# Scores and outputs in four 64x64 quarters of the array, whole-array work in six blocks of a batch

## The chip, the cores and the metric

One core of a Trainium2 chip. The metric is the device time of one execution in microseconds (us), median of several. Every run below fell in the fast state. Names of bursts: attention works through each batch in 16 **bursts**, u=0 to u=15, of two score tiles each; four **groups** of four bursts make a batch, one for each pair of heads and half of the queries. Names of tiles: `ps` holds scores, `p` their exponentials, `po` a group's outputs, `den` its denominators, `drow` a copy of them, `dcol` what is read back of them from DRAM; `c` is the column means in DRAM, `crow` their broadcast. A **step** is a piece of the next batch's work on TensorE (two graph matmuls, or a tile of keys or values).

## The reference, cut to what matters

Two layers, each with a residual and a layernorm. The change touches only the attention of the first, over 16 batches of 1024 nodes with 256 channels and 4 heads of 64, all in fp32:

```python
c_adj = jnp.mean(fea, axis=1)                      # column means of x
diff = c_adj[:, None, :] - c_adj[:, :, None]
A = jnp.abs(jnp.abs(jax.nn.sigmoid(diff) - 0.5) - 0.5) * 2.0
Wg = adj[None] * (A + A.T) * 0.5                   # the kernel: Abs, Tanh, times adj
g = relu(einsum('bcn,bnm->bcm', fea, Wg) * para)   # "graph": gives q
kv = x @ kv_w                                      # keys and values
attn = softmax(einsum('bhnd,bhmd->bhnm', q, k) * scale)
out = einsum('bhnm,bhmd->bhnd', attn, v)
x = layernorm(x + out)                             # then a graph layer, untouched here
```

## The kernel before

While a batch is in attention, the next batch's keys, values, graph products and weights (Abs/Tanh) are made beside it. The parts that matter (cuts marked):

```python
def begin():                      # once a batch: column means
    # ... csum = sum of x on VectorE, ccol and ncol from it
    nc.sync.dma_start(c_d[b].rearrange("o (n p) -> p (o n)", p=P), ncol)       # 1024 values of 4 bytes
    nc.sync.dma_start(s["crow"], c_d[b][0].partition_broadcast(P))

def graph_mm(c, half, part):      # ... 2 of 8 matmuls into pg
    if part == 3:
        nc.vector.scalar_tensor_tensor(q, ps, -scale, para_s[:, c, hs], op0=ALU.mult, op1=ALU.mult)
        nc.scalar.activation(q, q, AF.Relu)

def scores(i):                    # 64 rows x 128 columns of the array, two heads abreast
    for hd in range(2):
        r = slice(hd * D, (hd + 1) * D)
        nc.tensor.matmul(ps[:, hd * HALF : (hd + 1) * HALF], kT[r, pr, m * P : (m + 1) * P],
                         qT[r, pr, qh * HALF : (qh + 1) * HALF], start=True, stop=True)
    nc.scalar.activation(p, ps, AF.Exp)

def outputs(i):                   # 128 rows x 64 columns; acc is the sum of the p on VectorE
    # ...

def normalise(b, pr, qh):         # once a group: denominators
    # ... den = ones x acc, on TensorE
    nc.scalar.copy(row, den)
    for hd in range(2):
        nc.sync.dma_start(den_d[k][hd : hd + 1, :], row[hd * D : hd * D + 1, :])
    for hd in range(2):
        nc.sync.dma_start(col[:, :, hd], den_d[k][hd : hd + 1, :].rearrange("o (n p) -> p (o n)", p=P))
    nc.vector.reciprocal(r_all[:, k], col)

with tc.manual_schedule(engines={mybir.EngineType.PE}):
    for j in range(len(bursts)):
        # ... scores of j; one or two steps of the next batch; outputs of j - 1
```

The last statement matters below: only TensorE's instructions keep the order of the program. The order of the other engines, and of the DMAs that they issue, is laid out when the kernel is built.

Of the kernel before, what the change touches and what calls it, by code (L numbers as in the profile page):

```python
# [10 lines left out]
F32 = mybir.dt.float32  # L11
# [7 lines left out]
P = 128  # L19
HALF = 512  # L20
# [495 lines left out]
def fast_path(  # L516
# [42 lines left out]
    def tile_o(name):  # L559
        return ps_o.tile([P, HALF], F32, tag="o", name=name)  # L560
# [52 lines left out]
    with (  # L613
# [146 lines left out]
        def scores(i):  # L760
            b, pr, qh, m = units[i]
            qT, kT = st[b]["qT"], st[b]["kT"]
            ps = tile_s(f"ps_{i}")
            for hd in range(2):
                r = slice(hd * D, (hd + 1) * D)
                nc.tensor.matmul(  # L766
                    ps[:, hd * HALF : (hd + 1) * HALF], kT[r, pr, m * P : (m + 1) * P],
                    qT[r, pr, qh * HALF : (qh + 1) * HALF], start=True, stop=True,
                )
            p = pp.tile([P, N], F32, tag="p", name=f"p_{i}")  # L770
            nc.scalar.activation(p, ps, AF.Exp)  # L771
            A[i] = p

        def outputs(i):
            b, pr, qh, m = units[i]
            s, p = st[b], A.pop(i)
            if m == 0:
                G[b, pr, qh] = {
                    "po": tile_o(f"po_{i}"),
                    "acc": accp.tile([P, N], F32, tag="acc", name=f"acc_{i}"),  # L780
                }
            g = G[b, pr, qh]
            for hd in range(2):
                h = 2 * pr + hd
                nc.tensor.matmul(  # L785
                    g["po"][hd * D : (hd + 1) * D, :], s["v"][:, m, h * D : (h + 1) * D],
                    p[:, hd * HALF : (hd + 1) * HALF], start=(m == 0), stop=(m == NCH - 1),
                )
            if m == 0:
                g["p0"] = p  # L790
            elif m == 1:
                nc.vector.tensor_add(g["acc"], g.pop("p0"), p)
            else:
                nc.vector.tensor_add(g["acc"], g["acc"], p)  # L794

        def normalise(b, pr, qh):

            g = G[b, pr, qh]
            k = (b * PAIRS + pr) * 2 + qh
            den = tile_t(f"den_{k}")  # L800
            for hd in range(2):
                nc.tensor.matmul(
                    den[hd * D : (hd + 1) * D, :], ones,
                    g["acc"][:, hd * HALF : (hd + 1) * HALF], start=True, stop=True,
                )
            row = rdp.tile([P, HALF], F32, tag="drow", name=f"drow_{k}")
            nc.scalar.copy(row, den)
            for hd in range(2):
                nc.sync.dma_start(den_d[k][hd : hd + 1, :], row[hd * D : hd * D + 1, :])
            col = small.tile([P, 4, 2], F32, tag="dcol", name=f"dcol_{k}")  # L810
            for hd in range(2):
                nc.sync.dma_start(
                    col[:, :, hd], den_d[k][hd : hd + 1, :].rearrange("o (n p) -> p (o n)", p=P)
                )
            nc.vector.reciprocal(r_all[:, k], col)
            g["oT"] = op.tile([P, HALF], F32, tag="oT", name=f"oT_{k}")
            nc.scalar.copy(g["oT"], g["po"])

        def residual(b, pr, qh):
            g, s = G.pop((b, pr, qh)), st[b]  # L820
# [22 lines left out]



        BURST = 2
        bursts = [range(i, i + BURST) for i in range(0, len(units), BURST)]
        PERB = PER // BURST
        with tc.manual_schedule(engines={mybir.EngineType.PE}):
# [5 lines left out]
                run(steps, 2)  # L855
            next_first, next_steps, next_side = prologue(1)
            run(next_first, 4)
            full, cols64 = {}, {}

            def back(j):  # L860

                run(cols64.get(j, []), 9)
                for i in bursts[j]:
                    outputs(i)
                b, pr, qh, m = units[bursts[j][-1]]
                if m == NCH - 1:
                    cols64.setdefault(j + 1, []).append((normalise, (b, pr, qh)))
                    full.setdefault(j + 5, []).append((residual, (b, pr, qh)))

            for j in range(len(bursts)):  # L870
                b, u = j // PERB, j % PERB
                for i in bursts[j]:
                    scores(i)
                if u == 0:
                    steps, side = next_steps, next_side
                    next_first, next_steps, next_side = [], [], []
                run(full.get(j, []), 9)
                if u == 5 and b + 2 < B:
                    load_x(b + 2)
                    next_first, next_steps, next_side = prologue(b + 2)  # L880
                run(side, 3)
                run(steps, 1 + u % 2)
                if u >= 10:
                    run(next_first, 1)
                if u == PERB - 1:
                    run(steps, 99)
                if j:
                    back(j - 1)
            j = len(bursts)
            back(j - 1)  # L890
            for k in range(j, j + 6):
                run(cols64.get(k, []), 9)
                run(full.get(k, []), 9)

        top = l0c.tile([P, 2], F32, name="top")
# [276 lines left out]
```

## Time and profile before

| | before |
|---|---|
| time, median (range) | 2955.81 us (2954.03 to 2958.54) |
| TensorE busy | 2788.7 us, 94% |
| attention: first scores to last output transpose | 1754.3 us |
| in it: TensorE idle / changes of array shape | 11.5 us / 755 |

The last two rows are counted from the single TensorE records of the trace: the length between two records, the gaps between their ends and starts, and how often the recorded rows and columns change from one matmul to the next. The lines of the page stand in the prediction. The traced execution took 2962.3 us, a little over the range of the others, as it needed 89.0 us before the first scores (the trace after: 79.9); the comparisons of traces below are therefore of attention alone.

Two lines of the view of waits of the kernel before are needed later (engine, line, what it waited for; us in total, times, longest): ScalarE's relu of q waiting for VectorE's multiply, and VectorE's reciprocal waiting for the load of the denominators, which is next to nothing.

```profile
ACT qT L706 <- DVE qT L703: 136.5, 35, 7.1
DVE r_all L815 <- DMA dcol<-den: 3.8, 6, 1.9
```

### The profile page before, as it was taken

How to read it: one execution, taken by the hardware profiler on the slowest of the kernel's cores; microseconds unless marked ns; L12 is line 12 of the kernel's file. 1: busy time of each engine (PE TensorE's matmuls, PEld its weight loads, DVE VectorE, ACT ScalarE, POOL GpSimd, SP SyncE). 2: the span in 40 equal slices, each digit the busy share in tenths (PEclk: the TensorE clock that was granted, in tenths of full speed). 3: DMA queues.
4: the chain of work that ended last, by engine and by line, in shares of the span. 5: the costliest groups of instructions: out<-in, count | busy, mean ns of one | idle time of the engine just before them, and what ended most of it. 6: DMA issues, size and time to landing. Idle time of an engine off the chain costs nothing. (4 is left out here: it accounts for less than half of the span.)

```text
span 2960.4 us, 23733 instructions
## 1 busy us (share of the span) xinstructions
PE 2788.7 (94%) x9170; PEld 1178.5 (40%) x9170; DVE 1345.3 (45%) x2002; ACT 1143.4 (39%) x1313; POOL 222.8 (8%) x196
## 2 busy tenths in 40 slices
PE   5999999999999999999999999899999999999842
PEld 3433333333333333333333432644444444344432
DVE  3455654654654555655555646412111121333464
ACT  2553553553553553553554534001110111233383
POOL 0001001001001000100100101000000000000032
PEclk8999999999999999999999999699999999999955
DMA  4001101101101001001011011022212121243265
GB/s 135 8 1 36 29 8 36 30 8 36 29 8 37 29 8 37 16 21 37 8 29 36 1 35 38 29 85 114 85 57 86 71 85 57 104 165 142 85 213 200
DMA packets 122026, 168.42 MB, mean 57 GB/s; under 512 B 86704, under 2 KB 103600, under 8 KB 111664
## 3 DMA queue, kind: packets, MB, share of 16 engines
q1 hardware_dynamic: 112720, 99.70, 11.1%
q0 software_dynamic: 9184, 67.12, 5.7%
q8 instruction: 74, 1.21, 0.2%
q14 instruction: 48, 0.39, 0.0%
HBM read 99.36 MB, written 67.44 MB: 56 GB/s over the span
## 5 line engine op out<-in xcount | busy, mean ns | idle before, releaser
L771 ACT ACTIVATE p<-ps 128x1024 f32<-128x1024 f32 x512 | 497.5, 1020 | 406.2 <-PE ps L766 406.0
L794 DVE TENSOR_TENSOR acc<-acc,p 128x1024 f32<-128x1024 f32 x384 | 469.4, 1222 | 394.7 <-ACT p L771 377.6
L766 PE MATMUL ps<-qT,kT 64*128 64x512 f32 x2048 | 509.0, 615 | 0.1
L785 PE MATMUL po<-p,v 128*64 128x512 f32 x2048 | 492.5, 602 | 0.0
L697 PE MATMUL pg<-wg,x 128*128 128x512 f32 x1024 | 481.0, 606 | 2.8 <-ACT kT L718 2.6
L984 PE MATMUL pagg<-ahT,x1l 128*128 128x512 f32 x1024 | 444.1, 593 | 0.0
L1003 ACT ACTIVATE hw<-ph,col_b 128x1024 f32<-128x1024 f32 x64 | 71.3, 1114 | 651.4 <-PE ph L999 651.4
L766 PEld LDWEIGHTS ps<-qT,kT 64*128 64x128 f32 x2048 | 176.1, 186 | 327.7 <-issue 264.4
L984 PEld LDWEIGHTS pagg<-ahT,x1l 128*128 128x128 f32 x1024 | 194.4, 191 | 241.1 <-issue 241.1
L697 PEld LDWEIGHTS pg<-wg,x 128*128 128x128 f32 x1024 | 182.8, 190 | 269.4 <-issue 264.5
L785 PEld LDWEIGHTS po<-p,v 128*64 128x64 f32 x2048 | 129.8, 136 | 288.5 <-issue 288.2
L833 POOL TENSOR_TENSOR x<-x,o 128x512 f32<-128x512 f32 x64 | 118.2, 1846 | 1604.4 <-DVE o L828 1604.4
L1063 PE MATMUL po<-hl,w2T 128*128 128x512 f32 x512 | 222.8, 598 | 6.9 <-ACT hl L1054 6.9
L999 PE MATMUL ph<-agg,w1T 128*128 128x512 f32 x512 | 222.2, 592 | 0.0
L988 DVE COPY agg<-pagg 128x1024 f32<-128x1024 f32 x32 | 39.2, 1224 | 377.8 <-PE pagg L984 377.8
L685 DVE SCALAR_TENSOR_TENSOR wg<-wg,adj_s 128x1024 f32<-128x1024 f32 x128 | 157.0, 1248 | 74.8 <-ACT wg L684 74.8
L679 ACT ACTIVATE wg<-crow,ccol 128x1024 f32<-128x1024 f32 x128 | 141.2, 1141 | 35.5 <-PE pg L697 23.6
L1005 DVE BATCH_NORM_STATS2 bn_st<-hw 128x6 f32<-128x512 f32 x128 | 82.3, 685 | 152.4 <-ACT hw L1003 152.4
L1063 PEld LDWEIGHTS po<-hl,w2T 128*128 128x128 f32 x512 | 98.3, 192 | 131.5 <-issue 121.9
L999 PEld LDWEIGHTS ph<-agg,w1T 128*128 128x128 f32 x512 | 97.3, 190 | 122.5 <-issue 122.5
L1094 PE MATMUL pf<-ident,o 128*128 128x128 f32 x256 | 62.4, 421 | 83.4 <-DVE xf L1099 56.5
L727 PE MATMUL pv<-kvw_s,xT 128*128 128x256 f32 x512 | 126.5, 391 | 13.3 <-DMA kvw_s<-in_L_gnn_kv_w_dram 10.3
(85 smaller groups left out, 1855.3 us busy)
## 6 DMA issues: line engine op xcount, KB each, us to landing
h<-hw POOLq DMA_DIRECT2D x16, 2048.0 KB, 6.5
hl<-h SPq DMA_DIRECT2D x16, 2048.0 KB
x<-in_x_dram SPq DMA_DIRECT2D x16, 1024.0 KB
x<-x POOLq DMA_DIRECT2D x16, 1024.0 KB, 4.3
x1l<-x SPq DMA_DIRECT2D x16, 1024.0 KB
xf<-x SPq DMA_DIRECT2D x16, 1024.0 KB
out_dram<-xf POOLq DMA_DIRECT2D x16, 1024.0 KB, 5.4
crow<-c SPq DMA_DIRECT2D x16, 512.0 KB
```

The source lines that it names most:

```text
L679: nc.scalar.activation(w, s["crow"], AF.Abs, bias=s["ccol"][:, n : n + 1])
L685: nc.vector.scalar_tensor_tensor(w, w, 1.0, adj_s[:, n, :], op0=ALU.subtract, op1=ALU.mult)
L697: nc.tensor.matmul(ps, xt[:, n, c * P : (c + 1) * P], s["wg", n][:, hs], start=(n == 0), stop=(n == NCH - 1),)
L727: nc.tensor.matmul(pt[:, j * C : (j + 1) * C], s["xT"][:, c, n * P : (n + 1) * P], kvw_s[:, c, C : 2 * C], start=(c == 0), stop=(c == CC - 1),
L766: nc.tensor.matmul(ps[:, hd * HALF : (hd + 1) * HALF], kT[r, pr, m * P : (m + 1) * P], qT[r, pr, qh * HALF : (qh + 1) * HALF], start=True, ...
L771: nc.scalar.activation(p, ps, AF.Exp)
L785: nc.tensor.matmul(g["po"][hd * D : (hd + 1) * D, :], s["v"][:, m, h * D : (h + 1) * D], p[:, hd * HALF : (hd + 1) * HALF], start=(m == 0) ...
L794: nc.vector.tensor_add(g["acc"], g["acc"], p)
L833: nc.gpsimd.tensor_tensor(xs, xs, o.rearrange("p n h d -> p n (h d)"), ALU.add)
L984: nc.tensor.matmul(ps[:, hs], xt[:, m, c * P : (c + 1) * P], ahT[:, m, hs], start=(m == 0), stop=(m == NCH - 1),)
L999: nc.tensor.matmul(ps[:, hs], w1T[:, c, k * P : (k + 1) * P], t[:, c, hs], start=(c == 0), stop=(c == CC - 1),)
L1063: nc.tensor.matmul(ps[:, hs], w2T[:, k, c * P : (c + 1) * P], ht[:, k, hs], start=(k == 0), stop=(k == HC - 1),)
```

## The change

The intent: TensorE pays for changes between array shapes, so make scores, outputs and denominators one shape (64x64, four quarters at once), and put the work that needs the whole array into six blocks of a batch in place of a piece in every burst. The price is a second half of `den` and `po`, to be added.

```diff
 def scores(i):
-    for hd in range(2):
-        nc.tensor.matmul(ps[:, hd half], kT[r, pr, m * P : (m + 1) * P], ...)
+    for kh in range(2):
+        for hd in range(2):
+            ks = slice(m * P + kh * D, m * P + (kh + 1) * D)
+            nc.tensor.matmul(ps[kh * D : (kh + 1) * D, hd half], kT[r, pr, ks], ...)
 def outputs(i):                       # the same split; two tiles po[0], po[1]
+    if m == NCH - 1:
+        nc.scalar.copy(g["oT"], g["po"][0])
+        nc.vector.tensor_add(g["oT"], g["po"][1], g["oT"])
 def normalise(b, pr, qh):
-    den = tile_t(f"den_{k}")
+    den = [tile_t(f"den_{k}_{kh}") for kh in range(2)]     # four quarter matmuls
-    nc.scalar.copy(row, den)
+    nc.scalar.copy(row, den[0])
+    nc.vector.tensor_add(row, den[1], row)
+FULL = {1: 4, 4: 4, 6: 4, 9: 4, 11: 4, 14: 4}              # burst: steps of the next batch
 for j in range(len(bursts)):
     # scores(j)
+    run(quarter.get(j, []), 9)                             # normalise, now right after scores
-    run(steps, 1 + u % 2)
+    if u in FULL:
+        run(full.get(j, []), 9)                            # residuals
+        run(steps, FULL[u])
     # outputs(j - 1)
```

(Cut: the matmul arguments, and the placing of the residuals and of the transposes of x.)

More of the change, by code (lines that the diff above doesn't have):

```diff
@@ L763, in scores @@
             ps = tile_s(f"ps_{i}")
-            for hd in range(2):
-                r = slice(hd * D, (hd + 1) * D)
-                nc.tensor.matmul(
-                    ps[:, hd * HALF : (hd + 1) * HALF], kT[r, pr, m * P : (m + 1) * P],
-                    qT[r, pr, qh * HALF : (qh + 1) * HALF], start=True, stop=True,
-                )
+            for kh in range(2):
+                for hd in range(2):
+                    r = slice(hd * D, (hd + 1) * D)
+                    ks = slice(m * P + kh * D, m * P + (kh + 1) * D)
+                    nc.tensor.matmul(
+                        ps[kh * D : (kh + 1) * D, hd * HALF : (hd + 1) * HALF], kT[r, pr, ks],
+                        qT[r, pr, qh * HALF : (qh + 1) * HALF], start=True, stop=True,
+                    )
             p = pp.tile([P, N], F32, tag="p", name=f"p_{i}")
@@ L778, in outputs @@
                 G[b, pr, qh] = {
-                    "po": tile_o(f"po_{i}"),
+                    "po": [tile_o(f"po_{i}_{kh}") for kh in range(2)],
                     "acc": accp.tile([P, N], F32, tag="acc", name=f"acc_{i}"),
@@ L784, in outputs @@
                 h = 2 * pr + hd
-                nc.tensor.matmul(
-                    g["po"][hd * D : (hd + 1) * D, :], s["v"][:, m, h * D : (h + 1) * D],
-                    p[:, hd * HALF : (hd + 1) * HALF], start=(m == 0), stop=(m == NCH - 1),
-                )
+                for kh in range(2):
+                    r = slice(kh * D, (kh + 1) * D)
+                    nc.tensor.matmul(
+                        g["po"][kh][hd * D : (hd + 1) * D, :], s["v"][r, m, h * D : (h + 1) * D],
+                        p[r, hd * HALF : (hd + 1) * HALF], start=(m == 0), stop=(m == NCH - 1),
+                    )
             if m == 0:
@@ L794, in outputs @@
                 nc.vector.tensor_add(g["acc"], g["acc"], p)
+            if m == NCH - 1:
+                k = (b * PAIRS + pr) * 2 + qh
+                g["oT"] = op.tile([P, HALF], F32, tag="oT", name=f"oT_{k}")
+                nc.scalar.copy(g["oT"], g["po"][0])
+                nc.vector.tensor_add(g["oT"], g["po"][1], g["oT"])
         def normalise(b, pr, qh):
@@ L799, in normalise @@
             k = (b * PAIRS + pr) * 2 + qh
-            den = tile_t(f"den_{k}")
+            den = [tile_t(f"den_{k}_{kh}") for kh in range(2)]
             for hd in range(2):
-                nc.tensor.matmul(
-                    den[hd * D : (hd + 1) * D, :], ones,
-                    g["acc"][:, hd * HALF : (hd + 1) * HALF], start=True, stop=True,
-                )
+                for kh in range(2):
+                    r = slice(kh * D, (kh + 1) * D)
+                    nc.tensor.matmul(
+                        den[kh][hd * D : (hd + 1) * D, :], ones[r, :],
+                        g["acc"][r, hd * HALF : (hd + 1) * HALF], start=True, stop=True,
+                    )
             row = rdp.tile([P, HALF], F32, tag="drow", name=f"drow_{k}")
-            nc.scalar.copy(row, den)
+            nc.scalar.copy(row, den[0])
+            nc.vector.tensor_add(row, den[1], row)
             for hd in range(2):
@@ L815, in normalise @@
             nc.vector.reciprocal(r_all[:, k], col)
-            g["oT"] = op.tile([P, HALF], F32, tag="oT", name=f"oT_{k}")
-            nc.scalar.copy(g["oT"], g["po"])
         def residual(b, pr, qh):
@@ L857, in fast_path @@
             run(next_first, 4)
-            full, cols64 = {}, {}
+            full, quarter = {}, {}
             def back(j):
-                run(cols64.get(j, []), 9)
                 for i in bursts[j]:
@@ L866, in back @@
                 if m == NCH - 1:
-                    cols64.setdefault(j + 1, []).append((normalise, (b, pr, qh)))
-                    full.setdefault(j + 5, []).append((residual, (b, pr, qh)))
+                    quarter.setdefault(j + 2, []).append((normalise, (b, pr, qh)))
+                    k = j + 4
+                    while k % PERB not in FULL:
+                        k += 1
+                    full.setdefault(k, []).append((residual, (b, pr, qh)))
             for j in range(len(bursts)):
@@ L876, in fast_path @@
                     next_first, next_steps, next_side = [], [], []
-                run(full.get(j, []), 9)
                 if u == 5 and b + 2 < B:
@@ L881, in fast_path @@
                 run(side, 3)
-                run(steps, 1 + u % 2)
-                if u >= 10:
-                    run(next_first, 1)
-                if u == PERB - 1:
-                    run(steps, 99)
+                if u in FULL:
+                    run(full.get(j, []), 9)
+                    run(steps, FULL[u])
+                    if u >= 9:
+                        run(next_first, 1 if u < 12 else 2)
                 if j:
@@ L890, in fast_path @@
             back(j - 1)
-            for k in range(j, j + 6):
-                run(cols64.get(k, []), 9)
+            for k in range(j, j + 8):
+                run(quarter.get(k, []), 9)
                 run(full.get(k, []), 9)
```

## The prediction

> **What bounds the kernel now.** I read the page first (busy shares, the costliest groups, the idle time in front of each), then the TensorE timeline of one batch in the steady part, then the ScalarE and GpSimd timelines there. The chain that ended last covers only the last 12 us and says nothing of this change.
>
> The page: TensorE is busy in nine tenths or more of nearly every slice, and the two groups that the change rewrites never wait. The last column is the idle time before a group over the whole run.
>
> ```profile
> PE   5999999999999999999999999899999999999842
> PEclk8999999999999999999999999699999999999955
> L771 ACT ACTIVATE p<-ps 128x1024 f32<-128x1024 f32 x512 | 497.5, 1020 | 406.2 <-PE ps L766 406.0
> L766 PE MATMUL ps<-qT,kT 64*128 64x512 f32 x2048 | 509.0, 615 | 0.1
> L785 PE MATMUL po<-p,v 128*64 128x512 f32 x2048 | 492.5, 602 | 0.0
> ```
>
> The reader is to see 0.1 and 0.0 us of idle time: scores (L766) and outputs (L785) are bound by TensorE itself, while the exponential (ScalarE, L771) waited 406 us for it. So only TensorE's own time can be won here, and what other engines gain or lose counts only once they make it wait. Attention runs to about 1840 us of 2956; what follows is untouched.
>
> The timeline of TensorE over one burst with one "step" (columns: start, us, engine, line, operation, count):
>
> ```profile
> 1001.17 1.99 PE L766 MATMUL ps<-qT,kT 64*128 64x512 f32 x8
> 1003.08 1.98 PE L714 MATMUL pk<-xT,kvw_s 128*128 128x512 f32 x4
> 1005.00 1.94 PE L785 MATMUL po<-p,v 128*64 128x512 f32 x8
> 1006.87 1.99 PE L766 MATMUL ps<-qT,kT 64*128 64x512 f32 x8
> ...
> 1036.29 3.70 PE L697 MATMUL pg<-wg,x 128*128 128x512 f32 x8
> 1039.92 1.94 PE L785 MATMUL po<-p,v 128*64 128x512 f32 x8
> ```
>
> Each program matmul of 512 columns is recorded as two passes; within one block the next pass of the same tile starts 0.4295 us after the last (single starts in the trace: 1003.617, 1004.046, 1004.476). Scores and outputs already run two tiles abreast, so each of the three blocks is four rounds, 4 x 0.4295 = 1.718 us. But the starts are 1.91, 1.92 and 1.87 us apart: 5.70 us a burst for 5.154 us of rounds, 0.546 us lost at three changes of array shape (64x128, 128x128, 128x64). The wider block shows the contrast: 8 whole-array matmuls take 3.63 us, 1.71 more than 4 do, so staying in a shape costs nothing. By single starts: the first round after a change comes 0.09 us late, and its weight load delays the second round by 0.05 (64 columns) to 0.10 us (128 columns). **That is 0.19 us into the whole array, 0.145 into 128x64, 0.20 into 64x128.**
>
> A batch takes 112.6 us, from one residual add to the same one a batch later:
>
> ```profile
> 482.12 2.28 POOL L833 TENSOR_TENSOR x<-x,o 128x512 f32<-128x512 f32 x1 [17.29 <-DVE o L828]
> ...
> 594.74 2.31 POOL L833 TENSOR_TENSOR x<-x,o 128x512 f32<-128x512 f32 x1 [17.28 <-DVE o L828]
> ```
>
> Sum of its parts: scores 64 rounds, outputs 64, graph 64, keys 16, values 16, denominators 8 = 232 x 0.4295 = 99.6 us; transposes about 4 x 0.5 + 4 x 0.53 = 4.1; changes of shape 16 x 0.546 = 8.7. Together 112.4, so the account closes.
>
> **What the Trainium skill says.** (1) "TensorEngine Tiling (Array Packing)", Tiling Modes, Key Properties: "Changing tiling mode (not just tile) drains the TensorE". The trace agrees: 0.145 to 0.20 us per change, none between blocks of one shape. (2) "TensorE: Matmul & The Clock Gate", Part 3, Measured speedup vs the span model: tiles abreast cost one matmul plus some 4 ns per further tile. The trace agrees for two tiles (starts 1001.166 and 1001.173, and still 0.429 us to the next round); four tiles no trace here shows. (3) The same page, Part 2, LDWEIGHTS: its time goes with the columns, not the rows. The trace agrees: 186 ns for 64x128, 136 ns for 128x64. (4) "PSUM — Partial Sum Buffer", Specifications: eight banks of 512 fp32. The kernel holds 2 x 2 for scores, 2 for `t`, 2 for `o`: all eight. No trace shows that, but it is why each new double tile takes both buffers of its pool.
>
> **The change, part by part.** *Removed.* Quarters make scores and outputs one shape, and whole-array work stands in six blocks of a batch instead of in every burst. Forty-eight changes of shape a batch (8.7 us) become twelve: 6 x (0.19 + 0.145) = 2.0 us. Saved: 6.7 us a batch. The last batch has no steps, and its bursts take 3.79 us for 3.436 of rounds: 16 x 0.35 = 5.6 us saved less a little for residuals, some 5.
>
> *Unchanged if four tiles run abreast.* A unit's scores and outputs become four quarter matmuls each, still two rounds. Twice as many weight loads, each 64 columns at 0.136 us, beside rounds of 0.43: hidden, as now. Denominators: four quarters abreast, two rounds, as now.
>
> *Added off TensorE.* Per group (four a batch) one more VectorE add from PSUM for `po` and one for `den`, about 0.69 us each (128x512 from PSUM, as L828): 5.5 us on an engine busy 62.6 of 112.6. Hidden as work.
>
> *Added as waits.* (a) `den` now takes both `t` buffers. At u=1 and u=9 a whole-array block follows at once and needs one of them. From the start of the scores: exponentials begin 1.17 us later (1001.17 to 1002.34) and both are done at about 3.05; `den` ends at 1.72 + 0.86 = 2.58 plus 0.2 for its end to be seen, so the ScalarE copy runs 3.05 to 3.6, and TensorE, ready at 2.6, waits until 3.65: **1.1 us**, second buffer 0.1 more. At u=1 ScalarE is also making the next batch's weights, and an Abs or Tanh of 1 us may stand in front: I take 1.7. Sum 2.8 us a batch. (b) The two `po` tiles take both `o` buffers; the next group needs them 1.72 + 0.86 us later (scores and `den` lie between), while copy and add take 0.2 + 0.6 + 0.7 = 1.5. No wait, but for the group that ends at u=3, with the layernorm on VectorE: 0.4. (c) The second transpose of x at u=14 waits for the graph tile, 0.45, in place of today's 0.78 (the TensorE timeline has 0.78 before `den` at 1083.55): 0.3 gained. (d) ScalarE in bursts without a whole-array block: 3.44 us now hold two exponentials (1.85), and sixteen Abs and Tanh (16 us) become possible when the graph matmuls at u=14 free their buffers. The old timeline shows ScalarE mixing them in as soon as buffers come free:
>
> ```profile
> 1093.34 1.91 ACT L771 ACTIVATE p<-ps 128x1024 f32<-128x1024 f32 x2
> 1095.15 2.18 ACT L679 ACTIVATE wg<-crow,ccol 128x1024 f32<-128x1024 f32 x2
> 1097.23 1.99 ACT L684 ACTIVATE wg<-wg 128x1024 f32<-128x1024 f32 x2
> 1099.12 0.62 ACT L706 ACTIVATE qT<-qT 128x512 f32<-128x512 f32 x1
> 1099.64 2.18 ACT L679 ACTIVATE wg<-crow,ccol 128x1024 f32<-128x1024 f32 x2
> 1101.72 1.01 ACT L771 ACTIVATE p<-ps 128x1024 f32<-128x1024 f32 x1
> 1102.63 1.05 ACT L684 ACTIVATE wg<-wg 128x1024 f32<-128x1024 f32 x1
> 1103.57 1.01 ACT L771 ACTIVATE p<-ps 128x1024 f32<-128x1024 f32 x1
> ```
>
> An exponential may come one such operation late (that of 1101.72 did, by 1.1 us). The score buffers give 3.44 - 2.1 = 1.3 us of slack, and the six-block layout leaves ScalarE some 9 us at u=14 before the next exponentials. So nearly hidden: 0.2.
>
> *Sum.* 6.7 - 2.8 - 0.4 + 0.3 - 0.2 = 3.6 us a batch; 15 x 3.6 + 5 = 59 us, less 1 to 2 for two more evictions in the tail: 2956 - 57, about **2899**. I chose 2897, leaning a little to the side that some waits fall into gaps of the others.
>
> **The rivals.** *Waits (a) do not occur, or are shorter,* because the copy of `den` finds ScalarE free: for it, six blocks look placed with care; against it, the exponentials' timing above leaves it no earlier slot. Then 6.3 us a batch, some 2856. *ScalarE becomes the bound between u=14 and u=4:* exponentials queue behind several Abs and Tanh, as the order is fixed beforehand and the bursts got shorter, 3.44 us for 5.7 to 7.4. For it: six of these stand between two pairs of exponentials in the old timeline. Against it: they waited for buffers then, and only an order made for a slower TensorE would keep them so. It would cost 3 to 6 us a batch, so 2930 to 2985. *Four quarters do not run at full rate:* fp32 passes of four tiles start raggedly, or loads of weights collide. Five per cent on 136 quarter rounds of a batch are 2.9 us, 47 us in all: 2945. Against it: two tiles show a stagger of 7 ns and no loss[...]. *VectorE holds `p` too long* at u=4 with a layernorm of some 7 us: four `p` buffers give about 2.5 us of slack; at most 1 us a batch.
>
> **Range and chances.** The gain without new waits is firm (105 us: 2851). What the waits take back is some 45 us with an error about as large, to both sides; half-rate quarters would be far outside, but I hold them unlikely (one in ten for a loss that shows). So 2848 to 2948 eight times in ten. Two per cent is 2896.7 us, nearly my middle: faster 0.52, same 0.43, slower 0.05.
>
> **What would show it.** Right: scores and outputs as 64*64 groups of 4096 records each; pure bursts with starts 3.44 us apart; four starts within some 20 ns per round; TensorE's idle time naming the copy of `den` (L807's successor) before poT at u=1 and u=9, near 1 us each; a batch of about 109 us. Wrong: a round of quarters longer than 0.435 us; score matmuls idle behind the exponential by more than 1 us a batch; or whole-array blocks that lose much more than 0.335 us to their two changes. The prediction fails most likely through ScalarE's order, which I cannot read from the old trace.

## The result, and the profile after

| | before | after |
|---|---|---|
| time, median (range), four runs each | 2955.11 (2954.03 to 2958.54) | 3185.28 (3181.13 to 3186.38) |
| ratio, 95% interval | | 1.0774 (1.0755 to 1.0793): slower |
| attention | 1754.3 us | 1983.6 us |
| TensorE idle in it | 11.5 us | 248.1 us |
| TensorE busy at half clock in it | 0 | 139.1 us |
| changes of array shape | 755 | 189 |
| everything after attention | 1117.1 us | 1115.7 us |

Ratios are the mean time of one kernel's fast runs over that of the other's of the same rounds, so not quite the ratio of the medians quoted. (The kernel before has one run more here than in the first table.)

The page of the kernel after, against the lines in the prediction:

```profile
PEclk9999999998999999999999999969999999999955
L768 PE MATMUL ps<-qT,kT 64*64 64x512 f32 x4096 | 522.5, 621 | 148.7 <-ACT p L773 148.7
L789 PE MATMUL po<-p,v 64*64 64x512 f32 x4096 | 502.5, 603 | 4.9 <-DVE oT L803 4.9
```

The quarters are there, 4096 records each, and their busy time is near the old one's (522.5 and 502.5 us against 509.0 and 492.5). Single starts in the trace show four quarters at full rate: 1100.374, .378, .381 and .384 us, the next round 0.430 us on. But scores, which waited 0.1 us in all, now wait 148.7 us for the exponential.

The waits after, beside the two lines of before:

```profile
ACT qT L706 <- DVE qT L703: 532.5, 49, 19.9
DVE r_all L827 <- DMA dcol<-den: 204.5, 48, 9.9
PE ps L768 <- ACT p L773: 148.7, 53, 10.2
```

The reciprocal's wait went from 3.8 to 204.5 us, that of the relu from 136.5 to 532.5. The timeline of one batch shows how they hang together (start, us, engine, line, operation; in brackets the idle time before it and what ended it; SPq is the DMA queue that SyncE issues to):

```profile
1016.61 2.29 DVE L657 TENSOR_REDUCE csum<-x 128x8 f32<-128x2048 f32 x1 [5.72 <-DMA x<-in_x_dram]
...
1018.82 0.68 DVE L819 TENSOR_TENSOR drow<-den,drow 128x512 f32<-128x512 f32 x1
...
1019.52 0.54 SPq L821 DMA_DIRECT2D den<-drow  x2
...
1020.17 0.39 SPq L662 DMA_DIRECT2D c<-ncol  x1
...
1020.67 1.05 SPq L824 DMA_DIRECT2D dcol<-den  x2
...
1028.72 0.34 SPq L664 DMA_DIRECT2D crow<-c  x1
1031.70 0.20 DVE L827 RECIPROCAL r_all<-dcol 128x8 f32<-128x8 f32 x1 [9.60 <-DMA dcol<-den]
1031.82 0.64 DVE L703 SCALAR_TENSOR_TENSOR qT<-pg,para_s 128x512 f32<-128x512 f32 x1
1032.50 0.63 ACT L706 ACTIVATE qT<-qT 128x512 f32<-128x512 f32 x1 [18.98 <-DVE qT L703]
...
1034.09 3.56 PE L768 MATMUL ps<-qT,kT 64*64 64x512 f32 x16 [9.36 <-ACT p L773]
```

Read it from the bottom. TensorE stood 9.36 us for an exponential. On ScalarE a relu stood in front of it; the relu needed VectorE's multiply; on VectorE the reciprocal stood in front of that; and the reciprocal stood 9.60 us for the denominators, whose load (dcol) had been issued at 1020.67, 11.0 us earlier. Thirteen of the 16 batches have such a stall of TensorE, of 6.0 to 10.2 us, 108.2 of the 148.7 us in all. Two other groups of the same batch get their denominators 2.7 us after the issue (1045.70 to 1048.35, 1078.74 to 1081.48). What is different here is the store of the column means, c<-ncol, issued between the denominators' store and their load. The same stretch of the kernel before has it behind them:

```profile
1032.53 5.10 SPq L812 DMA_DIRECT2D dcol<-den  x2
...
1039.42 0.20 DVE L815 RECIPROCAL r_all<-dcol 128x8 f32<-128x8 f32 x1
...
1039.76 0.36 SPq L662 DMA_DIRECT2D c<-ncol  x1
...
1048.27 0.34 SPq L664 DMA_DIRECT2D crow<-c  x1
```

There, too, c<-ncol needs 8.5 us until the load behind it (crow) can be issued, but nobody else waits.

The other 40.5 us that scores wait, in 40 waits, have an Abs or a Tanh directly in front of the exponential on ScalarE, as here, where TensorE stood 1.83 us until 1094.02:

```profile
1091.93 1.13 ACT L679 ACTIVATE wg<-crow,ccol 128x1024 f32<-128x1024 f32 x1
1092.96 1.00 ACT L773 ACTIVATE p<-ps 128x1024 f32<-128x1024 f32 x1
```

One more thing is in the line at 1034.09: 16 records that take 1.90 us elsewhere take 3.56. The view of windows (the stretch, its length, busy time of PE, PEld, DVE, ACT and POOL with the number of records, then the granted clock, the DMA share and GB/s) shows the clock at half (0.50) after a stretch with idle time, here at u=0 of the next batch, where TensorE was busy 1.28 us of 3.40:

```profile
1092.00:1095.40 3.40, 1.28 (x12) 0.21 (x8) 2.87 (x4) 3.40 (x5) 0.00 (x0) 1.00 0.00 0
1095.40:1098.80 3.40, 2.93 (x16) 1.04 (x20) 2.92 (x3) 3.37 (x5) 0.00 (x0) 0.50 0.00 0
```

**The account of attention.** It is 229.3 us longer. Idle time explains 236.6. The 139.1 us of work at half clock would have taken half of that at full clock: 69.6 lost, an estimate. The remainder, 229.3 - 236.6 - 69.6 = -77 us, is put down to the 566 fewer shape changes: 0.136 us each.

### The profile page after: what moved, and what is told of

Same layout as the page of the kernel before. It is cut to its first block, busy times and chain, and to the rows that moved or that the text cites. A ratio compares the mean times of both kernels' runs of the same rounds, so it can differ in the third digit from the quotient of the medians.

```text
span 3179.2 us, 32796 instructions
## 1 busy us (share of the span) xinstructions
PE 2776.8 (87%) x13522; PEld 1213.2 (38%) x13522; DVE 1416.8 (45%) x2130; ACT 1139.3 (36%) x1313; POOL 213.8 (7%) x196
## 5 line engine op out<-in xcount | busy, mean ns | idle before, releaser
L768 PE MATMUL ps<-qT,kT 64*64 64x512 f32 x4096 | 522.5, 621 | 148.7 <-ACT p L773 148.7
L789 PE MATMUL po<-p,v 64*64 64x512 f32 x4096 | 502.5, 603 | 4.9 <-DVE oT L803 4.9
L697 PE MATMUL pg<-wg,x 128*128 128x512 f32 x1024 | 466.0, 609 | 20.7 <-DVE drow L819 17.1
L768 PEld LDWEIGHTS ps<-qT,kT 64*64 64x64 f32 x4096 | 155.5, 138 | 461.1 <-issue 233.3
L697 PEld LDWEIGHTS pg<-wg,x 128*128 128x128 f32 x1024 | 193.8, 194 | 272.8 <-issue 247.4
L789 PEld LDWEIGHTS po<-p,v 64*64 64x64 f32 x4096 | 152.0, 136 | 296.7 <-issue 286.1
L843 POOL TENSOR_TENSOR x<-x,o 128x512 f32<-128x512 f32 x64 | 109.0, 1704 | 1833.7 <-DVE o L838 1833.7
L706 ACT ACTIVATE qT<-qT 128x512 f32<-128x512 f32 x64 | 40.1, 626 | 532.5 <-DVE qT L703 532.5
L727 PE MATMUL pv<-kvw_s,xT 128*128 128x256 f32 x512 | 147.7, 439 | 57.5 <-DVE v L731 28.9
L727 PEld LDWEIGHTS pv<-kvw_s,xT 128*128 128x128 f32 x512 | 108.5, 220 | 100.8 <-DVE v L731 42.1
```

The lines of the kernel that those rows point to most:

```text
L697: nc.tensor.matmul(ps, xt[:, n, c * P : (c + 1) * P], s["wg", n][:, hs], start=(n == 0), stop=(n == NCH - 1),)
L727: nc.tensor.matmul(pt[:, j * C : (j + 1) * C], s["xT"][:, c, n * P : (n + 1) * P], kvw_s[:, c, C : 2 * C], start=(c == 0), stop=(c == CC - 1),
L768: nc.tensor.matmul(ps[kh * D : (kh + 1) * D, hd * HALF : (hd + 1) * HALF], kT[r, pr, ks], qT[r, pr, qh * HALF : (qh + 1) * HALF], start=Tr ...
L789: nc.tensor.matmul(g["po"][kh][hd * D : (hd + 1) * D, :], s["v"][r, m, h * D : (h + 1) * D], p[r, hd * HALF : (hd + 1) * HALF], start=(m = ...
L843: nc.gpsimd.tensor_tensor(xs, xs, o.rearrange("p n h d -> p n (h d)"), ALU.add)
```

## The experiments

Fifteen kernels. All were correct, all ran beside the kernel before on the same chip, three rounds each. "Gain" is against the 3185 us of the change. Theory 1, from the timeline above: VectorE's reciprocal holds up everything behind it. The rivals: it is TensorE's order of blocks, or ScalarE's Abs and Tanh; or the quarters themselves.

### e1: the reciprocal on GpSimd

```diff
-            nc.vector.reciprocal(r_all[:, k], col)
+            nc.gpsimd.tensor_tensor(r_all[:, k], col, mone, ALU.pow)     # mone: -1.0
```

> Only the reciprocal of the denominators moves from VectorE to GpSimd (power -1). Theory 1 (in order queues): in the changed kernel VectorE stands 9.6 us at this reciprocal for the denominators to come back from DRAM; the multiply that makes q is behind it, the relu of q behind that on ScalarE, and the exponentials behind the relu, so TensorE stands 9.4 us once a batch and then runs 3.4 us at half clock (about 11 us of a batch of 129). Then the reciprocal out of VectorE takes 15 x 11 = 165 us off 3185: 3000 to 3040, and the 9 us wait of the scores at u=7 is gone. Rival A (ScalarE is crowded by the next batch's Abs and Tanh): this wait is at u=15 and u=0 and is not touched; under 20 us of change. Rival B (both t buffers taken by the denominators): under 20 us of change.

3063.17 us (3061.54 to 3065.7), ratio 1.0362 (1.0344 to 1.0379): 122 us gained. Scores wait 41.3 us in place of 148.7, at most 1.8 at a time. The wait for the load moved to GpSimd, where TensorE no longer feels it. The middle of the chain is confirmed; the size is a miss, 122 us for an expected 145 to 185.

### e2: the six blocks at other bursts

```diff
-        FULL = {1: 4, 4: 4, 6: 4, 9: 4, 11: 4, 14: 4}
+        FULL = {2: 4, 4: 4, 6: 4, 10: 4, 12: 4, 14: 4}
```

> Only the places of the six whole-array blocks: 2, 4, 6, 10, 12, 14 for 1, 4, 6, 9, 11, 14, so that no block follows the denominators of the same burst. Rival B: the waits for the eviction of the two denominator tiles (0.83 + 1.14 us idle at u=1 and again at u=9, and 1.7 us of half clock at u=1, 5.6 us a batch) go: 85 us off 3185, about 3100. If that were the main cause it would go below 2990. Theory 1: the 9 us wait after the block at u=6 stays.

3134.74 us (3133.63 to 3140.5), ratio 1.0609 (1.0592 to 1.0627): 51 us gained. The wait of TensorE for `den`, at the head of the blocks u=1 and u=9, is gone, but keys now wait 26.2 us for VectorE's multiply of the outputs, so the gain is less than the 85 us expected. The long wait is not gone: scores still wait 157.1 us, the reciprocal 202.4. So the place of TensorE's blocks is a smaller part of the loss.

### e3 and e4: each half of the change alone

e3 has quarters for scores and outputs, with the old layout and the old `den`; e4 has the six blocks with the old shapes. (By the author's account, quarters for `den` as well, in the old layout, deadlocked at the build: the graph products hold one of the two `t` buffers, the PSUM tiles that they share with `den`, across bursts, and the double `den` needs both. No run on record shows it.)

> Quarters for scores and outputs alone (two po tiles, added at once on eviction), with the layout of the kernel before: a step in every burst, the denominators as one 128x64 tile. A burst changes shape twice (0.335 us) for three times (0.546 us), 3.4 us a batch less, four more changes into the denominators 0.6 us more: 2955 - 15 x 2.8 = about 2913 if quarters cost nothing by themselves. If quarters themselves are what is slow (rival C): above 2960. Rounds of quarters 0.43 us apart either way decide.

2988.58 us (2985.82 to 2991.01), ratio 1.0110 (1.0093 to 1.0127). A miss. The time lies where rival C was put, but the rounds, which were to decide, are 0.43 us apart (starts 1001.844 and 1002.273): the quarters run at full rate. No exponential is waited for (0.2 us), but values wait 27.4 us for VectorE and the graph products 18.3, and the reciprocal waited 178.5 us with at most 7.7 at a time. 557 shape changes stay.

> The six blocks alone, with the two old shapes and one tile each for po and den. Pure bursts change shape twice (0.345 us), bursts with a block three times (0.546): 6.7 us a batch for 8.7, 30 us less if nothing waits. Theory 1: the order of VectorE and the short bursts after a block are the layout's, so the wait behind the reciprocal comes here too, unless the denominators return sooner because ScalarE alone evicts them and nothing stands behind the sum over x: then a shorter one. I expect 3000 to 3100. Rivals B and C: no double tiles and no quarters, so 2925 to 2960.

3006.37 us (3003.59 to 3008.83), ratio 1.0172 (1.0155 to 1.0189). In range, without the long stall: the reciprocal waits 36.8 us, scores 16.2. In both halves, c<-ncol is issued after the denominators' load, as before the change: 2.4 to 3.1 us after it in e3, 3.4 to 3.8 in e4, about 7 before. Each half alone is slower than nothing, by 33 and 50 us; both together by 230, so most of the loss belongs to neither.

### e5, e6, e7: order on all engines

e5 takes quarters and blocks at e2's bursts and puts all engines, not only TensorE, in the order of the program, written so that nothing stands in front of what is more urgent: the reciprocal when the outputs are transposed, the sums of p right after the scores, the layernorm in three parts.

```diff
-        with tc.manual_schedule(engines={mybir.EngineType.PE}):
+        with tc.manual_schedule(engines=ENGINES):          # PE, Activation, DVE, Pool, SP
-            nc.vector.reciprocal(r_all[:, k], col)         # in normalise
+            nc.vector.reciprocal(r_all[:, k], g["col"])    # in residual
```

> Quarters and six blocks kept (at 2, 4, 6, 10, 12, 14, clear of the denominators); all engines and the DMA queue follow the program's order, written so that nothing that waits long stands in front of the exponentials: the reciprocal comes with the residual that uses it, the sums of p right after the scores, the layernorm in three parts, eight of the sixteen Abs and Tanh inside the block at u=14. Theory 1 (the loss is order, not shape): TensorE's idle time in the attention falls from 248 us to under 40 and the half clock goes (139 us busy at half clock, 70 us lost), so 3185 - 280 = 2880 to 2905, faster than the kernel before. Rival (short bursts are too much for ScalarE or VectorE whatever their order): scores go on waiting for exponentials, above 2955.

2909.12 us (2907.2 to 2912.1), ratio 0.9843 (0.9827 to 0.9859). A miss by 4 us, and the first that beats the kernel before.

e6 is e1 and e2 together:

> The two single changes of before together: reciprocal on GpSimd and the blocks at 2, 4, 6, 10, 12, 14, order otherwise left to the automatic scheduling. If they are independent: 3185 - 122 - 50 = 3013. What is left must be the waits at u=15 and u=0 for exponentials behind Abs and Tanh (41 us idle and some half clock), and those for VectorE at u=4.

2969.9 us (2966.62 to 2973.38), ratio 1.0047 (1.0030 to 1.0063): 215 us gained, more than the 173 of the two alone. The trace says where the rest comes from: e2's new wait of keys, 26.2 us, isn't there, and only 28.4 us of work run at half clock, against 112.6 in e1 and 92.3 in e2. With the reciprocal on another engine and the blocks at other bursts, the change nearly breaks even.

e7 is e5 with the old shapes of scores, outputs and denominators:

> As e5, with the old shapes of scores, outputs and denominators (64x128 and 128x64, one po and one den tile). If quarters are worth what the changes of shape cost: 10 bursts x 0.345 + 6 x 0.21 = 4.7 us a batch more than e5, some 70 us: 2950 to 2975. If quarters bring nothing by themselves: within 15 us of e5.

2960.3 us (2958.26 to 2962.79), ratio 1.0012 (1.0006 to 1.0019), as expected. Between two kernels in the same order, quarters are worth 51 us.

### e8 and e11: mending e5

e5 still lost 20 us once, before the first exponentials, as eight Abs and Tanh of the second batch stood ahead. e8 mends the start (the diff), and moves the Abs and Tanh of u=15, 0 and 1 into the block at u=2; within the block at u=14 the last relu comes behind the fourth pair of Abs and Tanh:

```diff
-            while steps:
-                run(side, 4)
-                run(steps, 2)
-            next_first, next_steps, next_side = prologue(1)
-            run(next_first, 5)
-            run(next_side, 8)
+            run(steps, 8)
+            run(side, 16)
+            next_first, next_steps, next_side = prologue(1)
+            run(next_first, 1)
+            run(steps, 16)
+            run(next_first, 4)
```

> As e5 with three places of its order mended: before the first scores only the batch's own Abs and Tanh (e5 had eight of the next batch there, and TensorE stood 20 us once, then ran at half clock); all Abs and Tanh inside the blocks at u=14 and u=2, none in the short bursts; the relu after the fourth pair. The start gives about 25 us, and a batch goes from 107.3 to about 106 (0.83 us of wait at u=0 and 0.45 at u=1 gone), 15 x 1.3 = 20 us: 2909 - 45 = 2855 to 2880, and over 2% faster than the kernel before.

2907.8 us (2903.55 to 2907.9), ratio 0.9833 (0.9817 to 0.9850): a miss. The start was mended, but keys now wait 28.3 us for VectorE's multiply of the outputs, which e5 does not have. e11 therefore takes the start alone, the diff above and nothing else:

> The kernel in program order (2909 us) with its start alone mended as in the second program-order kernel (2908 us): the Abs/Tanh of the first batch run before the next batch's, and eight of them are no longer ahead of the first exponential. The start gave 9 us there (first scores at 82.3 instead of 91.4 us) plus a 20 us stall less, and the two other edits gave it back as waits for the keys. If so: 2880 to 2895 us. If instead the start only moves the same wait to the next batch: 2900 to 2910 us.

2874.47 us (2872.84 to 2876.38), ratio 0.9726 (0.9710 to 0.9743): faster than the kernel before by 81 us, and better than expected. The fastest version found. Its page:

```profile
L769 PE MATMUL ps<-qT,kT 64*64 64x512 f32 x4096 | 503.0, 591 | 11.9 <-ACT p L774 11.9
L800 PE MATMUL po<-p,v 64*64 64x512 f32 x4096 | 506.9, 594 | 0.5 <-DVE oT L808 0.4
```

TensorE is idle 13.4 us in all of attention, against 11.5 before the change, and never at half clock.

### e9: who makes the denominators late

Theory 1 began with the addition of the two halves of `den`, queued on VectorE behind the sum of x (1016.61 and 1018.82 above). e9 takes it off VectorE.

```diff
-            nc.vector.tensor_add(row, den[1], row)
+            nc.scalar.copy(row1, den[1])
+            nc.gpsimd.tensor_tensor(row, row, row1, ALU.add)
```

> The changed kernel with one thing undone: the second half of the denominators is evicted by ScalarE too and the halves are added on GpSimd, so VectorE is not on their way. Theory 1, its first link (the 9 us wait comes because this add stands on VectorE behind the sum over x, which waits for the load of x, so that the denominators leave and return late): the wait of VectorE at the reciprocal falls from 204 us to under 60 and the scores' long wait at u=7 goes, though the reciprocal stays on VectorE: 3040 to 3080, as in e1. If the DMA itself is what is slow there, or the doubled tiles are: above 3150.

3133.55 us (3132.32 to 3133.94), ratio 1.0600 (1.0583 to 1.0618): a miss. TensorE's long wait is still there, 9.80 us, and the reciprocal's waits grew to 243.2 us. So this first link of theory 1 is wrong. (e9 gains 52 us all the same, though not there: 60.5 us of work run at half clock in place of 139.1, and TensorE idles 13 us less.) The trace has dcol issued at 996.30 us, 0.42 us after c<-ncol, and the reciprocal at 1007.23.

### e10 and e12: the store of the column means on another queue

Theory 3 (so numbered in the record): dcol is late because c<-ncol stands ahead of it on SyncE's queue.

```diff
-                nc.sync.dma_start(c_d[b].rearrange("o (n p) -> p (o n)", p=P), ncol)
+                nc.gpsimd.dma_start(c_d[b].rearrange("o (n p) -> p (o n)", p=P), ncol)
-                nc.sync.dma_start(s["crow"], c_d[b][0].partition_broadcast(P))
+                nc.gpsimd.dma_start(s["crow"], c_d[b][0].partition_broadcast(P))
```

> The changed kernel with two DMAs moved: the column means' store (c<-ncol, 1024 packets of 4 bytes, once a batch) and their broadcast load (crow<-c) are issued from GpSimd's queue in place of SyncE's. In the changed kernel's trace SyncE issues c<-ncol between the store of the denominators (den<-drow) and their load (dcol<-den), and dcol then takes 11.0 us from issue to the reciprocal, against 2.7 to 4.6 us for the three other groups of a batch; the crow load, which needs nothing but c<-ncol, is issued 8.05 us after dcol's issue, in the kernel before 8.5 us after c<-ncol. Theory 3 (the long wait of the reciprocal is the small-packet store ahead of it on the same queue): the longest wait of the reciprocal in this stretch falls from 9.6 to about 2 us, its waits in total from 204 to under 110 us, the 9.4 us stall of the scores shrinks to 1 to 3 us a batch and most half-clock stretches after it go; 13 such groups x 8 us plus the half clock: 3040 to 3075 us. Theory 1 as it stood (the reciprocal waits because VectorE and ScalarE made the denominators late, and the queue is beside the point): 3170 to 3190 us, unchanged.

3193.21 us (3192.86 to 3197.35), ratio 1.0810 (1.0792 to 1.0828): nothing gained. The timeline:

```profile
1023.64 0.93 POOL L662 DMA_DIRECT2D c<-ncol  x1 [12.45 <-DVE ncol L661]
...
1024.37 0.95 SPq L824 DMA_DIRECT2D dcol<-den  x2
...
1035.02 0.20 DVE L827 RECIPROCAL r_all<-dcol 128x8 f32<-128x8 f32 x1 [9.22 <-DMA dcol<-den]
```

The store left the queue, and dcol, alone on it, took 10.7 us all the same. The queue is not the cause; that the two are under way at the same time still may be. The Trainium skill, "DMA: Bandwidth & Descriptors", section "Issuing engines are not separate DMA queues", says that DMAs of all issuing engines run on the same 16 DMA engines and interleave there. This trace fits it, as a store on another queue delays the load just as much (10.7 us for 11.0); which engine moved what, it does not show.

> The changed kernel with both edits: the two column-mean DMAs on GpSimd's queue, and the reciprocal of the denominators on GpSimd (as in the run that took 3063 us). If both act on the same wait (a late dcol holding up VectorE), the sum of the two gains does not appear: 3010 to 3060 us, little under the better of the two alone. If they act on different waits, the gains add: below 2960 us.

3061.4 us (3052.2 to 3063.01), ratio 1.0349 (1.0332 to 1.0366): e1's time, as e10 changed nothing. It doesn't decide what it was meant to.

### e13: the same store in fewer packets

The same 4 KB at the same place, in 128 pieces of 32 bytes in place of 1024 of 4. The means then land in another order, a fault made on purpose (the result stayed within the tolerance).

```diff
-                nc.sync.dma_start(c_d[b].rearrange("o (n p) -> p (o n)", p=P), ncol)
+                nc.sync.dma_start(c_d[b].rearrange("o (p n) -> p (o n)", p=P), ncol)
```

> The changed kernel with the store of the column means (c<-ncol, 4 KB, once a batch) written in 32-byte pieces, 128 of them, in place of 1024 of 4 bytes; the means then land in another order, so the result may be wrong, on purpose. Moving that store to another queue changed nothing (3193 us): the load of the denominators still took some 10 us from issue to the reciprocal whenever the store had been issued within 1 us of it. Theory 3b (the small packets of the store hold the DMA engines[...], so the load of the denominators waits 8 us whichever queue carries it): the longest reciprocal waits fall from 9.6 to about 2 us, the 9.4 us stall of the scores nearly goes, 3040 to 3090 us. Rival (something else delays that load, such as the 1 MB load of x just before it): 3175 to 3195 us.

3050.6 us (3046.68 to 3057.06), ratio 1.0319 (1.0302 to 1.0336): 135 us gained by two letters that change places. The timeline:

```profile
1080.22 0.35 SPq L662 DMA_DIRECT2D c<-ncol  x1
1080.74 0.93 SPq L824 DMA_DIRECT2D dcol<-den  x2
1081.78 0.44 SPq L664 DMA_DIRECT2D crow<-c  x1
...
1083.50 0.20 DVE L827 RECIPROCAL r_all<-dcol 128x8 f32<-128x8 f32 x1 [1.32 <-DMA dcol<-den]
```

The order of the DMAs is that of the kernel after, and the 1 MB load of x stands before them as there. The store is done within 1.56 us of its issue (when crow, which needs it, is issued) in place of 8.55, and dcol is used 2.76 us after its issue in place of 11.0. Scores wait 49.9 us in place of 148.7, and none of the 13 long stalls is left:

```profile
PE ps L768 <- ACT p L773: 49.8, 50, 2.6
```

This settles what makes the load late: the store in 4-byte pieces. It is not that these pieces keep the DMA engines busy, as the expectation had it. The view of DMAs of the kernel after (busy tenths in 40 slices of 1019 to 1033 us) has all of them through by 1023.2 us, and no packet moves until 1030.9, while the reciprocal stands until 1031.70. Nor is it the number of packets: in e10 the trace has the store in 32 of them, and the load was as late. So the delay comes after the packets, in the landing or in its notice; which, and why, no run here shows.

```profile
DMA  0000007626330000000000000000000000975992
```

### e14: the reciprocal later in the program

The reciprocal is written in the residual, as in e5, with the order of the engines left to the build.

> The changed kernel with one edit: the reciprocal of the denominators is taken in the block that transposes the group's outputs, at least two bursts later, in place of right after its load is issued; it stays on VectorE. In the kernel in program order this place and the order went together; here the order is left as the changed kernel has it. Theory 1 as mended (what costs is that VectorE stands in front of a load that is late, with the q multiply, the relu and the exponentials behind it): as the reciprocal on GpSimd, 3050 to 3080 us. If the order of the other engines matters more than the place of the reciprocal: above 3130 us.

3191.81 us (3185.37 to 3196.27), ratio 1.0794 (1.0776 to 1.0812): nothing gained. It isn't evidence against theory 1, since the trace shows that the reciprocal did not move. It stands where it stood, with the q multiply behind it:

```profile
1036.51 0.20 DVE L832 RECIPROCAL r_all<-dcol 128x8 f32<-128x8 f32 x1 [9.37 <-DMA dcol<-den]
```

Presumably the build puts it where it expects its inputs to be ready; that isn't shown. A place in the program text is an order only for engines that are held to it; the edit tested nothing else.

### e15: what the quarters alone are worth

e11 with the old shapes (the edits of e7).

> The fastest version so far (program order with the mended start, 2874 us) with the old shapes of scores, outputs and denominators. The difference is what the quarters are worth where nothing waits: 415 fewer shape changes by 0.135 us are 56 us, so 2925 to 2945 us. If the old shapes wait more or less than the quarters, it falls outside.

2926.89 us (2926.06 to 2927.25), ratio 0.9904 (0.9888 to 0.9921), as expected. e11 was run in another call, whose runs of the kernel before agree with these within 0.6 us. The difference to it is 52 us: 49.7 us of attention, in which e11 idles 6.0 us more, so 55.7 us for 415 shape changes, 0.134 each.

## Why the prediction was wrong

The account of attention, by the prediction's own parts (us over all batches; predicted parts times 15 batches, as in the prediction's sum, the first plus 5 for the last batch; measured from the waits of the kernel after and the account above):

| part of the sum | predicted | measured |
|---|---|---|
| fewer changes of shape | -105 | -77 |
| (a) `den` takes both buffers | +42 | +63 (outputs' transposes 26.5, graph 17.1, values 19.7) |
| (b) `po` takes both buffers | +6 | +5, by luck: one wait of 4.9 in the last batch, none at u=3 |
| (c) transpose of x at u=14 | -4.5 | -6 (11.0 of before gone, 5.1 new) |
| (d) exponentials late through ScalarE's order | +3 | +149 (108 in 13 long stalls, 40 behind Abs and Tanh) |
| values wait for VectorE's copies of v | not foreseen | +25 |
| work at half clock | not foreseen | +70 |
| two more evictions in the tail | +1 to 2 | not measured |
| sum | about -57 | +229 |

**What held.** TensorE was the bound. Four quarters run at full rate. Fewer changes of shape save time, but mostly less than the 0.186 us that the prediction's 6.7 us for 36 changes comes to: 0.134 from e15 to e11, 0.15 from before to e11 (83.4 us less attention with 1.9 us more idle time, so 85.3 us for 566 changes). It is no constant. From before to e15 (33.7 us less attention, 4.1 less idle, 151 changes fewer) it is 0.20. The same account for e3 (attention 31.9 us longer, 45.8 more idle, 5.5 lost at half clock, 198 changes fewer) leaves 0.10 us a change, and e4's 120 fewer changes leave nothing that shows (50.4 us longer, 50.9 more idle). Term (a) had the right mechanism and place; it was mis-sized, 2.8 us a batch for 4.0, because I counted the ScalarE copy and left out VectorE's addition after it: the second buffer costs 1.1 to 1.4 us (17.1 / 15 and 19.7 / 14), not 0.1. The first copy alone was put well, 26.5 us in 32 waits, 0.83 each for "near 1 us".

**The step that failed is (d), "nearly hidden: 0.2" us a batch.** Measured are 9.3 us a batch (148.7 / 16), and the prediction's own sign of being wrong, scores idle behind the exponential by more than 1 us a batch, came true. The rival named there, "ScalarE becomes the bound", exponentials behind several Abs and Tanh, is what happened in 40.5 of the 148.7 us, 2.5 us a batch for its "3 to 6". For the other 108.2 it saw the right engine in front of TensorE and the wrong reason: Abs and Tanh are not what stands in front in the long stall. ScalarE waits itself (18.98 us), for VectorE, which waits for a DMA. I had called VectorE's additions "hidden as work" from its busy time (62.6 of 112.6 us), and the busy time says nothing of an engine that stands still with others queued behind it. The chain, of which links 2 and 3 are shown by experiments and 1 and 4 read from the traces:

1. The column means' store and the denominators' load come to be issued within 0.6 us of each other. In 13 of 16 batches it happens in the kernel after and in e1, e2, e6, e9, e13 and e14 (in e10 and e12 within 0.9 us), which all have quarters and blocks and leave the order to the build, and never in e3, e4 or before. What in the combination sets this order was not isolated; e9 shows that it isn't the addition on VectorE, and e2 that it isn't the place of the blocks.
2. The store's 1024 pieces of 4 bytes delay the load by some 8 us (e13), whichever queue carries the store (e10).
3. The reciprocal stands in front of VectorE for that time, the multiply behind it holds the relu, and the relu the exponentials (the timeline; e1 breaks this link and gains 122 us, e13 the one before and gains 135).
4. TensorE stands for 9.4 us and starts again at half clock (16 records in 3.56 us for 1.90).

**The half clock** was missing from my working. Waits are paid for again: 70 us in all. The long stalls are the smaller part of that: with them gone (e13), 95.8 of the 139.1 us at half clock are still there. The skill, "TensorE: Matmul & The Clock Gate", Part 1, has the clock fall to half after an idle window of some 3.4 us; here much shorter waits sufficed (last section). Any wait of a microsecond or two in my sum should have carried that question. e11, with next to no idle time, shows none of it.

**And the gain was real.** With the waits taken away it appears: e11 is 2874 us, 23 us under my 2897 and 23 over the 2851 that I had called firm. Not all of that is the change: e15 has e11's order without the quarters and is at 2927, so the order and the blocks give some 28 us and the quarters 52.

What stays open: e13 is still 95 us above the kernel before. That is (a), 63 us, the values' waits, 25, the exponentials, 50, and the 48 us lost of 95.8 at half clock, less the 77 of the shapes. (a) is gone in e2 and e6; the waits for values and for exponentials behind Abs and Tanh (28.1 and 48.6 us in e6) went only with e5's order, in which many places changed at once.

## What to carry to other kernels

Before shortening the bound engine, follow each other engine's queue in order, and ask which of its instructions waits for a DMA and what stands behind it: slack in busy time is no slack for a queue that is blocked at its head. Here a store in 1024 four-byte pieces delayed a small load that somebody waited for by 8 us, from either queue; larger pieces cured it, and a load issued 2.4 us before the store (e3) was not held up. And if a layout depends on a fine order on several engines, fix the order on all of them, and look in the trace whether an edit moved the instruction at all.

## What the Trainium skill lacked or had wrong

- "TensorE: Matmul & The Clock Gate", Part 1: it gives an idle window of about 3.4 us as what drops the clock. In the kernel after, a stretch of 3.40 us in which TensorE was busy for 1.28 us, with 1.83 us as its longest gap, was followed by one at clock 0.50; a window need not be idle throughout. (A later passage of the page lets short gaps between matmuls do it too, without a figure.) Counted over the trace's clock records in windows of 3.413 us, every window at full clock that was followed by half clock (43) had TensorE busy for 46% or less, and every one that was not (753) for 42% or more. The length of this slow stretch agrees, 3.4 us.
- "DMA: Bandwidth & Descriptors": it has a figure for the overhead of a small packet itself, and none for how long a store in small pieces holds up the completion of another DMA. Here a 4 KB store in 4-byte pieces took 8.5 us (in the batch shown) and made a 4 KB load issued beside it 8 us late; in 32-byte pieces it took 1.6 us and delayed nothing that shows.
- "TensorEngine Tiling (Array Packing)", Tiling Modes, Key Properties: it says that a change of mode drains TensorE and gives no figure. The runs show 0.13 to 0.20 us a change between whole layouts, 0.10 in e3, and nothing that shows in e4.
- "TensorE: Matmul & The Clock Gate", Part 3: its table of measured packings has no case of four 64x64 tiles. Here four fp32 quarters start 3 to 4 ns apart and repeat every 0.430 us, in the kernel after.
